# Three expert weight buffers with six gather and twelve sample buffers, in place of two, ten and eight

## The chip, the cores and the metric

The kernel runs on one NeuronCore of a Trainium2 chip. The metric is the device time of one execution in microseconds (us). Ten executions of the kernel before have a median of 6801.84 us and lie between 6792.43 and 6807.85 us.

Five engines work side by side, each through its own instruction queue, in order: PE (TensorE, matrix products and transposes), DVE (VectorE), ACT (ScalarE), POOL (GpSimd, which here issues the indirect DMAs) and SP (SyncE, which issues the plain DMAs). An instruction waits on semaphores for what it needs, and everything behind it on its engine waits with it.

## The reference

Input `x` is (4, 256, 64, 64) in float32. One layer is computed:

```python
x = x + conv_stack(layernorm_over_channels(x))      # three layers, each:
    om   = conv3x3(x, w_off) + b_off                # 27 channels: 18 offsets, 9 masks
    samp = bilinear(x, grid + offsets) * sigmoid(mask)   # 9 taps per position
    x    = relu(einsum('bikhw,oik->bohw', samp, w) + b)  # 9 taps x 256 channels -> 256
t = tokens(x)                                       # (4, 4096, 256)
t = t + ffn(layernorm(t))                           # 8 experts, the best two of each token:
    probs = softmax(t @ gate_w + gate_b); top-2 weights
    y_e   = gelu(t @ W1[e] + b1[e]) @ W2[e] + b2[e]      # 256 -> 512 -> 256
    out   = sum over the two experts of weight * y_e
```

The reference runs all eight experts over all tokens. The kernel runs an expert only on the tokens that chose it.

## The kernel before

**Stages.** A convolution layer of one image is a stage; there are twelve, in the order written out in `run`. A stage has 8 blocks of 512 positions, a block 9 taps, a tap 4 gathers of 128 positions: 288 gathers a stage, 3456 in all. For each gather (`samples`), POOL issues an indirect DMA that brings 128 rows of 4 KB into a gather buffer `g` (L503); DVE makes two weighted sums (L509, then L514 into a sample buffer `s`); ACT scales `s` in place (L517). Two samples are a pair. In `turn`, PE transposes a pair into PSUM (L532) and ACT copies it to `sT` (L535); in `finish`, PE multiplies the four samples of a tap by that tap's weights (L555). A gather buffer is free again when L514 has read it, a sample buffer when PE has transposed it. There are ten of the first (`GB`) and eight of the second (pool `smp`).

**Experts.** When the tokens of an image (a group; the last image has two) are ready, `route` sorts them by expert and cuts them into tiles of 256, so that each tile has one expert: `NF` tiles, 39 for a full group and 23 for a half one, 163 in all. `expert` works one tile off in three pieces. Piece 1: `products` of the tile before (DVE adds the bias that lies in the weight buffer, L892), then PE transposes the tile's tokens (L840) and ACT copies them (L844). Piece 2: first product on PE (L856), and gelu on ACT with a bias that also lies in the weight buffer (L866). Piece 3: second product on PE (L874). At the start of piece 3 (`if beside`), `fetch_next` has POOL issue three indirect DMAs for the next tile: its weights `w` (L800) and two halves of its tokens `zt` (L812). When the kernel drains a lane between or after stages (`self.draining`), the call stands at the start of piece 2 instead. `ffn`, the pool of `zt`, has two buffers.

The weights take 9,232 bytes in each of 128 partitions. If a tile has the same expert as its predecessor, its row numbers are put out of bounds (`same`, L751 to L755) and the DMA moves nothing. The list is walked as two lists, its first half and its second (`order`): even steps take tiles from the first and use weight buffer 0, odd steps from the second, buffer 1.

**Pace.** Lanes mix the pieces into the taps: in a group of pace 5.0 (the first two) a tile goes into 5 taps, at 2.0 into 2 taps, at 1.5 into 1.5; the last group has pace 0. A third lane, `sums`, adds the two expert results to the tokens of the group before: two indirect DMAs `gy` (L915) and two DVE sums (L930) for each 128 tokens. The Tile layer below places each instruction in its engine's order and adds the semaphore waits.

While stage 0 is prepared, `room` also lends gather buffers to the blocks of the input (`xc`, `h`). The `wt` pool, whose two buffers later hold expert weights, lends windows then.

Of the kernel before, what the change touches and what calls it, by code (L numbers as in the profile page):

```python
# [34 lines left out]
FT_LOG = 8  # L35
FT = 1 << FT_LOG
FU = FT // P
GB = 10
LAG = 2
LEAST = 2.0**-30  # L40
WINN = CC * (RPB + 2) * W
W1N = CC * HID + HC
W2N = HC * C + C
# [39 lines left out]
class Group:  # L83


    def __init__(self, b, n0, n1):
        self.b, self.n0, self.n1 = b, n0, n1
        self.nm = f"{b}_{n0}"
        self.M = (n1 - n0) * TPB

        self.NF = 2 * self.M * P // FT + E - 1


        self.half = (self.NF + 1) // 2
        self.zt, self.acc, self.gy, self.sums, self.py = {}, [], [], [], None
        self.order = [s // 2 + s % 2 * self.half for s in range(self.NF)]


class Lane:
# [18 lines left out]
class Weave:  # L118
# [3 lines left out]
    def __init__(self, ctx, tc, ins, out):  # L122
        nc = self.nc = tc.nc
        self.tc = tc
        self.ins = ins
        self.x = ins["x"].rearrange("b (c p) h w -> b p c (h w)", p=P)
        self.out_v = out.rearrange("b (c p) h w -> b p c (h w)", p=P)
        self.B = self.x.shape[0]

        def pool(name, bufs, **kw):  # L130
            return ctx.enter_context(tc.tile_pool(name=name, bufs=bufs, **kw))

        self.cst = pool("cst", 1)
        self.dram = pool("dram", 1, space=bass.MemoryType.DRAM)
        self.wkp = pool("wkp", 1)
        self.plan = pool("plan", 19)
        self.win = pool("win", 3)
        self.wt = pool("wt", 2)
        self.small = pool("small", 1)
        self.big = pool("big", 2)  # L140
        self.ffn = pool("ffn", 2)
        self.rt = pool("rt", 1)
        self.rt2 = pool("rt2", 2)
        self.gyp = pool("gyp", 4)
        self.smT = pool("smT", 2)
        self.smp = pool("smp", 8)
        self.gat = pool("gat", GB)
        self.ps = pool("ps", 3, space=bass.MemoryType.PSUM)
        self.ps1 = pool("ps1", 1, space=bass.MemoryType.PSUM)

        self.routes, self.tiles, self.sums = Lane(), Lane(), Lane()
        self.side, self.plans_side = [], []
        self.last = self.gathered = self.turned = None
        self.starting, self.draining, self.later = True, False, []
        self.pend, self.pairs = None, []
# [534 lines left out]
    def route(self, grp):  # L690

        nc, M, NF = self.nc, grp.M, grp.NF
        grp.slots = self.rt2.tile([P, 2, M], I32, tag="slots", bufs=3, name=f"slots_{grp.nm}")
        grp.tok = self.rt2.tile([P, FU * NF], I32, tag="tok", name=f"tok_{grp.nm}")
        grp.wrow = self.rt2.tile([P, NF], I32, tag="wrow", name=f"wrow_{grp.nm}")

        def small(tag, shape, dt=F32):
            return self.rt.tile(list(shape), dt, tag=tag, name=f"{tag}_{grp.nm}")

        both = small("r0", (P, E, M))  # L700
        nc.vector.tensor_scalar(both, grp.rk, 1.0, None, ALU.is_le)
        rp = self.ps.tile([P, 2, E, M], F32, tag="tp", name=f"rp_{grp.nm}")
        nc.tensor.matmul(rp[:, 0], lhsT=self.upper, rhs=both, start=True, stop=True)
        nc.tensor.matmul(rp[:, 1], lhsT=self.ones, rhs=both, start=True, stop=True)
        tot = small("r1", (P, E, M))
        nc.vector.tensor_copy(tot, rp[:, 1])
        slot = small("r2", (P, E, M))
        nc.vector.tensor_tensor_scan(
            slot.rearrange("p e m -> p (e m)"),
            self.fresh[M].rearrange("p e m -> p (e m)"),  # L710
            tot.rearrange("p e m -> p (e m)"),
            0.0, ALU.mult, ALU.add,
        )

        ni = small("ni", (P, E), I32)
        nc.vector.tensor_scalar(ni, slot[:, :, M - 1], float(FT - 1), None, ALU.add)
        nc.vector.tensor_scalar(ni, ni, FT_LOG, None, ALU.logical_shift_right)
        nt = small("nt", (P, E))
        nc.vector.tensor_copy(nt, ni)
        end = small("end", (P, E))  # L720
        nc.vector.tensor_tensor_scan(end, self.ones[:, :E], nt, 0.0, ALU.mult, ALU.add)
        off = small("off", (P, E))
        nc.vector.tensor_tensor(off, end, nt, ALU.subtract)
        nc.vector.tensor_scalar(off, off, float(FT), None, ALU.mult)
        nc.vector.tensor_tensor(slot, slot, tot, ALU.subtract)
        nc.vector.tensor_tensor(slot, slot, rp[:, 0], ALU.add)
        nc.vector.tensor_tensor(
            slot, slot, off.unsqueeze(2).to_broadcast([P, E, M]), ALU.add
        )
        for i in range(2):  # L730
            mine = small("r0", (P, E, M))
            nc.vector.scalar_tensor_tensor(
                mine, grp.rk, float(i), slot, ALU.is_equal, ALU.mult
            )
            sf = small("sf", (P, M))
            nc.vector.tensor_reduce(sf, mine.rearrange("p e m -> p m e"), AX.X, ALU.add)
            nc.vector.tensor_copy(grp.slots[:, i, :], sf)

        past = small("r1", (P, NF, E))
        nc.vector.tensor_tensor(  # L740
            past,
            self.row_f[:, :NF].unsqueeze(2).to_broadcast([P, NF, E]),
            end.unsqueeze(1).to_broadcast([P, NF, E]),
            ALU.is_ge,
        )
        ex = small("ex", (P, NF))
        nc.vector.tensor_reduce(ex, past, AX.X, ALU.add)
        nc.vector.tensor_scalar(ex, ex, float(E - 1), None, ALU.min)

        rows = small("rows", (P, NF))  # L750
        nc.vector.tensor_scalar(rows, ex, float(P), self.part, ALU.mult, ALU.add)  # L751
        same = small("same", (P, NF))
        nc.vector.tensor_tensor(same[:, 1:], ex[:, 1:], ex[:, : NF - 1], ALU.is_equal)
        nc.vector.memset(same[:, 0 : grp.half + 1 : grp.half], 0.0)
        nc.vector.scalar_tensor_tensor(rows, same, float(E * P), rows, ALU.mult, ALU.add)  # L755
        nc.vector.tensor_copy(grp.wrow, rows)


        grp.digits = []
        for v, (op, k) in enumerate(((ALU.bitwise_and, P - 1), (ALU.logical_shift_right, 7))):  # L760
            di = small("di", (P, 2, M), I32)
            nc.vector.tensor_scalar(di, grp.slots, k, None, op)
            df = small(f"df{v}", (P, 2, M))
            nc.vector.tensor_copy(df, di)
            grp.digits.append(df)
        grp.inv = self.ps1.tile([P, FU * NF], F32, tag="py", name=f"inv_{grp.nm}")
# [23 lines left out]
    def fetch(self, grp, step):  # L790

        if self.w is None:
            self.w = [
                self.wt.tile([P, 2, WINN], F32, tag="wt", name=f"w_{i}").rearrange(
                    "p a b -> p (a b)"
                )
                for i in range(2)
            ]
        f = grp.order[step]
        self.nc.gpsimd.indirect_dma_start(  # L800
            out=self.w[step % 2][:, : W1N + W2N],
            out_offset=None,
            in_=self.ins["W"],
            in_offset=bass.IndirectOffsetOnAxis(ap=grp.wrow[:, f : f + 1], axis=0),
            bounds_check=E * P - 1,
            oob_is_err=False,
        )
        grp.zt[step] = []
        for u in range(FU):
            zt = self.ffn.tile([P, C], F32, tag=f"zt{u}", name=f"zt_{grp.nm}_{f}_{u}")  # L810
            j = FU * f + u
            self.nc.gpsimd.indirect_dma_start(  # L812
                out=zt,
                out_offset=None,
                in_=grp.zd,
                in_offset=bass.IndirectOffsetOnAxis(ap=grp.tok[:, j : j + 1], axis=0),
            )
            grp.zt[step].append(zt)
# [6 lines left out]
    def expert(self, grp, step):  # L825

        nc = self.nc
# [3 lines left out]
        self.products(grp)  # L831
        f = grp.order[step]
        nm = f"{grp.nm}_{f}"
        w = self.w[step % 2]
        w1, w2 = w[:, :W1N], w[:, W1N : W1N + W2N]
        zt = grp.zt.pop(step)
        tp = self.ps.tile([P, CC, FT], F32, tag="tp", name=f"ftp_{nm}")
# [6 lines left out]
        nc.scalar.copy(zT, tp)  # L844
        yield

        beside = not self.draining
        if not beside:
            self.fetch_next(grp, step)
        hT = []  # L850
        for h0 in range(0, HC, 2):
            ph = self.ps1.tile([P, 2, FT], F32, tag="ph", name=f"ph_{nm}_{h0}")
# [13 lines left out]
                nc.scalar.activation(ht[:, h, :], ph[:, h, :], AF.Gelu, bias=w1[:, k : k + 1])  # L866
            hT.append(ht)
        yield
        if beside:
            self.fetch_next(grp, step)  # L870
        py = self.ps1.tile([P, FU, C], F32, tag="py", name=f"py_{nm}")
        for u in range(FU):
            for h in range(HC):
# [262 lines left out]
```

## Time and profile before

The profiled execution took 6800.73 us; its span, from the first to the last instruction, is 6799.0 us.

| what | before |
|---|---|
| median of ten executions | 6801.84 us |
| profiled execution, its span | 6800.73 us, 6799.0 us |
| mean granted TensorE clock | 0.979 |
| PE busy | 6210.4 us (91%) |
| DVE busy | 4963.1 us (73%) |
| ACT busy | 3281.1 us (48%) |
| POOL busy | 4446.6 us (65%), of it L503 3649.4 us |
| DMA | 2223.73 MB; 327 GB/s in the mean |
| weight DMAs issued, of which moved data | 163, 45 |

The 45 are counted from the DMA packets of 9,232 bytes: 5,760, at 128 to a load. "Busy" is time in which an engine executes; "waited for" names what ended its idle time. An engine that idles costs nothing unless the work that it delays is on the path that sets the end.

The stages, as the start of the first gather of each shows them, begin at 93, 614, 1055, 1502, 1961, 2459, 2978, 3508, 4052, 4564, 5074 and 5771 us; the last gather is consumed at 6375 us. Tiles of experts run from 2165 us on: the two groups of pace 5.0 beside stages 4 to 9, that of pace 2.0 beside stage 10, that of pace 1.5 beside stage 11, and the last from 6216 us to about 6740 us.

### The profile page before, as it was taken

How to read it: one execution, taken by the hardware profiler on the slowest of the kernel's cores; microseconds unless marked ns; L12 is line 12 of the kernel's file. 1: busy time of each engine (PE TensorE's matmuls, PEld its weight loads, DVE VectorE, ACT ScalarE, POOL GpSimd, SP SyncE). 2: the span in 40 equal slices, each digit the busy share in tenths (PEclk: the TensorE clock that was granted, in tenths of full speed). 3: DMA queues.
4: the chain of work that ended last, by engine and by line, in shares of the span. 5: the costliest groups of instructions: out<-in, count | busy, mean ns of one | idle time of the engine just before them, and what ended most of it. 6: DMA issues, size and time to landing. Idle time of an engine off the chain costs nothing.

```text
span 6799.0 us, 88985 instructions
## 1 busy us (share of the span) xinstructions
PE 6210.4 (91%) x26500; PEld 3521.5 (52%) x26500; DVE 4963.1 (73%) x11467; ACT 3281.1 (48%) x7141; POOL 4446.6 (65%) x4245
## 2 busy tenths in 40 slices
PE   7998888889999999999999999999998899988987
PEld 3443344444445555555554555555555565755665
DVE  7887778778999676668889777667878555688511
ACT  3554455555555445445554444545554444454322
POOL 4664766766667666666667777666666666677643
PEclk8999999999999999999999999999999999999998
DMA  8998999999999999999998999989998887899744
GB/s 289 349 352 302 365 355 369 357 348 389 382 393 351 329 351 336 322 336 348 356 364 309 363 360 376 322 327 340 353 347 308 290 292 271 293 350 334 245 137 125
DMA packets 800319, 2223.73 MB, mean 327 GB/s; under 512 B 104728, under 2 KB 302872, under 8 KB 794080
## 3 DMA queue, kind: packets, MB, share of 16 engines
q0 software_dynamic: 551200, 1947.35, 77.8%
q1 hardware_dynamic: 248640, 270.69, 11.8%
q8 instruction: 215, 3.52, 0.2%
q14 instruction: 264, 2.16, 0.1%
HBM read 2160.68 MB, written 196.40 MB: 347 GB/s over the span
## 4 chain that ended last, share of the span: by engine, by line
PE 71%; ACT 8%; DMA 7%; DVE 6%; issue 4%; POOL 3%; SPq 0%; ACTq 0%; DVEq 0%; POOLq 0%
PE acc L555 36%; PE tp L532 10%; PE ph L856 7%; PE py L874 7%; PE po L357 7%; DMA g<-tab,idx 5%; ACT sT L535 3%; DVE g L509 2%; ACT s L517 2%; DVE s L514 2%; POOL g L503 1%; POOL gy L915 1%; PE pm L371 1%; ACT win L577 1%; PE ftp L840 1%
## 5 line engine op out<-in xcount | busy, mean ns | idle before, releaser
L503 POOL DMA_INDIRECT g<-tab,idx x3456 | 3649.4, 1056 | 1792.7 <-DVE s L514 642.7
L555 PE MATMUL acc<-sT,wk 128*128 128x512 f32 x6912 | 3386.7, 604 | 151.9 <-ACT sT L535 137.1
L509 DVE SCALAR_TENSOR_TENSOR g<-g,cf 128x512 f32<-128x512 f32 x3456 | 2560.9, 743 | 393.1 <-DMA g<-tab,idx 388.5
L514 DVE SCALAR_TENSOR_TENSOR s<-g,cf 128x256 f32<-128x256 f32 x3456 | 1661.7, 483 | 753.5 <-PE tp L532 469.0
L535 ACT COPY sT<-tp 128x512 f32<-128x512 f32 x1728 | 1001.4, 586 | 1820.8 <-PE tp L532 1814.0
L517 ACT ACTIVATE s<-s,cf 128x256 f32<-128x256 f32 x3456 | 1641.2, 508 | 435.0 <-DVE s L514 398.3
L555 PEld LDWEIGHTS acc<-sT,wk 128*128 128x128 f32 x6912 | 1161.0, 192 | 967.0 <-issue 655.4
L532 PEld LDWEIGHTS tp<-ident,s 128*128 128x128 f32 x6912 | 882.4, 143 | 1350.8 <-issue 651.2
L532 PE MATMUL tp<-ident,s 128*128 128x128 f32 x6912 | 1252.8, 281 | 189.3 <-ACT s L517 171.8
L856 PE MATMUL ph<-fzT,w 128*128 128x256 f32 x2608 | 682.6, 394 | 60.6 <-ACT fzT L844 36.1
L874 PE MATMUL py<-w,hT 128*128 128x256 f32 x2608 | 653.1, 389 | 31.3 <-ACT hT L866 26.1
L856 PEld LDWEIGHTS ph<-fzT,w 128*128 128x128 f32 x2608 | 481.4, 195 | 188.0 <-ACT fzT L844 63.5
L874 PEld LDWEIGHTS py<-w,hT 128*128 128x128 f32 x2608 | 475.2, 192 | 164.7 <-ACT hT L866 69.1
L866 ACT ACTIVATE hT<-ph,w 128x256 f32<-128x256 f32 x652 | 282.2, 471 | 455.9 <-PE ph L856 436.8
L812 POOL DMA_INDIRECT zt<-z,tok x326 | 334.6, 1026 | 161.1 <-issue 86.1
L357 PE MATMUL po<-win,wo 128*32 128x504 f32 (+1 forms) x2304 | 356.6, 597 | 5.5 <-ACT win L301 3.2
L800 POOL DMA_INDIRECT w<-in_W,wrow x163 | 176.7, 1084 | 268.0 <-issue 97.7
L915 POOL DMA_INDIRECT gy<-ys,slots x256 | 262.2, 1024 | 109.8 <-issue 63.0
L892 DVE TENSOR_TENSOR y<-py,w 128x512 f32<-128x512 f32 x163 | 111.7, 685 | 220.6 <-PE py L874 220.6
L930 DVE SCALAR_TENSOR_TENSOR ta<-gy,cw,ta 128x256 f32<-128x256 f32 x256 | 120.6, 480 | 135.9 <-DMA gy<-ys,slots 77.1
L357 PE MATMUL po<-win_pre,wo 128*32 128x504 f32 (+1 forms) x1152 | 185.3, 621 | 2.0 <-ACT om L366 2.0
L357 PEld LDWEIGHTS po<-win,wo 128*32 128x32 f32 x2304 | 73.0, 109 | 177.0 <-issue 141.7
(154 smaller groups left out, 2927.9 us busy)
## 6 DMA issues: line engine op xcount, KB each, us to landing
tab<-hv SPq DMA_DIRECT2D x512, 128.0 KB
g<-tab,idx POOLq DMA_INDIRECT x3456
ys<-y SPq DMA_DIRECT2D x163, 256.0 KB
tab<-h_pre SPq DMA_DIRECT2D x128, 256.0 KB
wk<-in_conv_w SPq DMA_DIRECT2D x99, 256.0 KB
xc_pre<-in_x SPq DMA_DIRECT2D x32, 512.0 KB
xr_tok<-in_x SPq DMA_DIRECT2D x32, 512.0 KB
t<-t_tok SPq DMA_DIRECT2D x32, 512.0 KB
```

What stands on the lines that cost most here:

```text
L357: nc.tensor.matmul(po[g * Q : (g + 1) * Q, :].rearrange("q (r w) -> q r w", w=W)[:, :, x0:x1], lhsT=self.wo[l][:, 3 * ky + kx, c, :], rhs= ...
L503: self.gathered = nc.gpsimd.indirect_dma_start(out=g.rearrange("p x s f -> p (x s f)"), out_offset=None, in_=self.table(*self.stages[i]), ...
L509: nc.vector.scalar_tensor_tensor(g[:, :, 0, :], g[:, :, 1, :], cf[:, j, 0:1], g[:, :, 0, :], ALU.mult, ALU.add,)
L514: self.last = nc.vector.scalar_tensor_tensor(s, g[:, 1, 0, :], cf[:, j, 1:2], g[:, 0, 0, :], ALU.mult, ALU.add)
L517: nc.scalar.activation(s, s, AF.Copy, scale=cf[:, j, 2:3])
L532: self.turned = nc.tensor.transpose(tp[:, c, u * P : (u + 1) * P], ss[u][:, c * P : (c + 1) * P], self.ident)
L535: nc.scalar.copy(self.sT[:, :, t0 * P : (t0 + 2) * P], tp)
L555: nc.tensor.matmul(acc[:, o, :], lhsT=self.wk[k][:, c, o * P : (o + 1) * P], rhs=sT[:, c, :], start=(k == 0 and c == 0), stop=(k == K - 1 ...
L812: self.nc.gpsimd.indirect_dma_start(out=zt, out_offset=None, in_=grp.zd, in_offset=bass.IndirectOffsetOnAxis(ap=grp.tok[:, j : j + 1], axi ...
L856: nc.tensor.matmul(ph[:, h, :], lhsT=w1[:, o : o + P], rhs=zT[:, c, :], start=(c == 0), stop=(c == CC - 1),)
L874: nc.tensor.matmul(py[:, u, :], lhsT=hT[h // 2][:, h % 2, u * P : (u + 1) * P], rhs=w2[:, h * C : (h + 1) * C], start=(h == 0), stop=(h == ...
L915: self.nc.gpsimd.indirect_dma_start(out=g, out_offset=None, in_=self.ys[grp.i % 3], in_offset=bass.IndirectOffsetOnAxis(ap=grp.slots[:, i, ...
```

## The change

The list of a group's tiles is walked as three thirds instead of two halves, with a weight buffer for each; the row numbers are valid again at the start of each third. `fetch_next` is called at the start of piece 2 always. The gather buffers go from ten to six, the sample buffers from eight to twelve.

```diff
-GB = 10
+GB = 6
@@ class Group
-        self.half = (self.NF + 1) // 2
+        self.third = -(-self.NF // 3)
-        self.order = [s // 2 + s % 2 * self.half for s in range(self.NF)]
+        self.order = [s // 3 + s % 3 * self.third for s in range(self.NF)]
@@ class Weave
-        self.wt = pool("wt", 2)
+        self.wt = pool("wt", 3)
-        self.smp = pool("smp", 8)
+        self.smp = pool("smp", 12)
@@ def route
-        nc.vector.memset(same[:, 0 : grp.half + 1 : grp.half], 0.0)
+        nc.vector.memset(same[:, 0 : 2 * grp.third + 1 : grp.third], 0.0)
@@ def fetch
-                for i in range(2)
+                for i in range(3)
-            out=self.w[step % 2][:, : W1N + W2N],
+            out=self.w[step % 3][:, : W1N + W2N],
@@ def expert
-        w = self.w[step % 2]
+        w = self.w[step % 3]
@@ def expert, start of piece 2
-        beside = not self.draining
-        if not beside:
-            self.fetch_next(grp, step)
+        self.fetch_next(grp, step)
@@ def expert, start of piece 3
-        if beside:
-            self.fetch_next(grp, step)
```

In bytes of a partition, four gather buffers less are 16,384, four sample buffers more 4,096, and the third buffer of the `wt` pool 10,240.

## The prediction

> **What bounds the kernel now.** I read the busy shares first (PE 91%, DVE 73%, POOL 65%), then the busy times by stage, because the mean hides that the stages differ, and then the waits inside the stages that stand out. Columns of the first view: stretch in us, its length, busy time and instructions of PE, PEld, DVE, ACT and POOL, granted clock, DMA share, GB/s.
>
> ```profile
> 582.00:1064.00 482.00, 420.60 (x1683) 189.68 (x1681) 360.95 (x742) 232.29 (x514) 311.52 (x295) 0.99 0.92 341
> 1513.00:1975.00 462.00, 422.86 (x1793) 221.22 (x1793) 426.24 (x1134) 247.96 (x547) 315.13 (x290) 0.97 1.01 387
> 5090.00:5746.00 656.00, 591.88 (x2539) 371.66 (x2537) 428.07 (x946) 297.71 (x636) 432.77 (x413) 0.96 0.84 295
> 5746.00:6375.00 629.00, 583.94 (x2505) 381.17 (x2505) 455.80 (x1069) 306.32 (x642) 436.68 (x415) 0.98 0.89 318
> 6375.00:6799.00 424.00, 337.87 (x1506) 266.09 (x1504) 96.67 (x262) 96.58 (x214) 186.63 (x191) 0.89 0.45 138
> ```
>
> PE is the bound nearly everywhere. Stage 3 (second line) has three engines near full at once: PE 92%, DVE 92%, DMA 1.01. In stages 10 and 11 (third and fourth) PE idles 109.2 of 1285 us, 8.5%; in stages 4 to 9 (1975 to 5090 us, PE busy 2939.3) it idles 175.7 of 3115, 5.6%. The waits of stages 10 and 11 say why; the last two lines are from the tail after 6375 us.
>
> ```profile
> DVE g L509 <- DMA g<-tab,idx: 283.2, 145, 10.5
> POOL w L800 <- ACT s L517: 52.7, 18, 4.8
> POOL w L800 <- ACT hT L866: 30.7, 10, 5.2
> POOL w L800 <- ACT sT L535: 13.2, 5, 4.4
> ...
> PE ph L856 <- DMA w<-in_W,wrow: 20.7, 7, 7.5
> PE ftp L840 <- DMA zt<-z,tok: 3.1, 2, 1.8
> ```
>
> DVE waits for gathers (283 of its 388 us in the whole run), and POOL is held at the weight DMA. All rows of L800 there but "issue" sum to 124 us over 40 waits, 3.1 each. The timeline shows one:
>
> ```profile
> 5335.67 0.95 POOL L503 DMA_INDIRECT g<-tab,idx  x1 [0.30 <-issue]
> ...
> 5337.86 0.75 DVE L509 SCALAR_TENSOR_TENSOR g<-g,cf 128x512 f32<-128x512 f32 x1 [7.08 <-DMA g<-tab,idx]
> ...
> 5343.97 0.68 DVE L892 TENSOR_TENSOR y<-py,w 128x512 f32<-128x512 f32 x1
> ...
> 5345.44 1.47 POOL L800 DMA_INDIRECT w<-in_W,wrow  x1 [4.75 <-ACT s L517]
> ```
>
> POOL cannot issue the weight DMA until DVE has read the bias out of that buffer (5343.97); eight gathers and two gy are queued behind it.
>
> **The third buffer and the earlier fetch.** At pace 2.0 a tile step takes 20.1 us (21 steps from 5324 to 5747) and POOL issues 13 DMAs in it: 8 gathers, w, two zt, two gy, at 0.96 + 0.30 us, 16.4 us. With the wait of 3 to 4.75 us this is the step. PE needs 592/656 of it, 18.1 us. So POOL's wait, not PE, sets the step.
>
> With two buffers, the fetch for tile s+1 waits for L892 of tile s-1: two pieces back, 1.3 taps or 5 gathers at pace 2.0. With three it waits for tile s-2, four pieces back even though it is issued a piece earlier. In the built programs the instruction waited for stands some 35 places ahead of the DMA before, over 170 after. zt, now the nearer wait (L840 of tile s-1, four pieces back instead of five), has two buffers still; four pieces at pace 1.5 are two taps, 8 gathers. I take both as free while POOL's lead is at most 6. What that relief is worth: if stages 10 and 11 idle like stages 4 to 9, 1175.8/0.9436 = 1246 us, **-39 us**; the bounds are 0 and -109, all of PE's idle time there. That the lead is then held by the gather buffers instead keeps me from going above -39.
>
> In the tail, fetch_next stood at piece 2 already; only the buffer counts. A load that moves data is issued when L892 of s-2, not s-1, is done: a tile earlier, and a tile there takes 8.2 us (L892 at 6507.03, 6515.23, 6523.42). The longest wait is 7.5, so all should go: **-24 us** (20.7 + 3.1). Bounds: 0 (zt waits for L840, 48.0 us on POOL, stand in front of w in the queue) and -40, with PE's weight-load waits of 12.6 and 3.6 counted as separate.
>
> In stages 4 to 9 POOL's largest row at L800 is 15.4 us of "issue", in 49 waits: nothing to gain.
>
> **Thirds.** Each group has one more break, so up to 5 loads more than 45, each 128 packets of 348 ns on 16 engines, 2.8 us: 14 us of DMA. A load now has three pieces of lead (16 us at pace 2.0). **+3 us**, bounds 0 and 14; without that cover it is PE at L856 that waits. The other DMAs of a step and the memset are unchanged in number.
>
> **Six gather buffers.** Gather j now waits for L514 of gather j-6; behind it on POOL stand the next gathers, w, zt and gy, and DVE waits for those. I took, for each of the 3456 gathers, its issue, its landing (its semaphore's last update) and its consumption. Issue to landing is 6.7 us at the median, 5.1 at the fast end (5%), 10.0 at 95%. A turn of one buffer is 0.3 + 6.7 + 1.3 (L509 0.74, L514 0.48) = 8.3 us; over six buffers 1.4 us per gather, against a cadence of 1.55 (stages 1 and 2) to 2.3 us (stage 10). So it holds in the mean, barely. Stage 3 has a mean landing of 8.25: (8.25 + 1.6)/6 = 1.64 against 1.59; it does not hold there.
>
> [...]
>
> How much a late gather costs: moving each issue to 0.25 us after the consumption of j-6 and keeping its landing time, 840 gathers land after DVE asked, in 171 runs of neighbours; adding only the largest delay of each run, DVE is late by 244 us in all. Most is covered: in stages 0, 1, 2, 5, 8 and 9 DVE finishes a sample 9.1 to 10.6 us (median) before ACT scales it, and 0 to 3.5 us per stage come through. In stages 3, 4 and 6, where that slack is 1.4, 8.7 and 4.7, 25.2 + 8.2 + 6.2 come through: **+39 us**. The 11 us of the other stages I leave to the four samples more. One place in stage 10 (5246 us, 26 us) I leave out: DVE was held there by full sample buffers, and it now has four more. Bounds: 0, and 244 if no cover holds.
>
> **Twelve sample buffers.** They let DVE run four further ahead: DVE waits 469 us at L514 for PE to free a sample. Up to the first expert tiles the built order of PE and ACT is the same as before, and ACT there waits for PE, not DVE. I take **0**, as what keeps the cover above; bounds -44 (a third of the 131 us that PE waits for ACT's s outside stages 10 and 11) and 0. Together ten plus eight and six plus twelve hold the same 18 gathers between POOL and PE.
>
> **The start.** Fewer lent buffers: SP's loads wait for buffers used three blocks earlier. Taken at 0; bounds 0 and +9, one round from load to load (24.12 to 33.16 us).
>
> **Sum.** 6800.7 - 39 - 24 + 3 + 39 = 6780 us for the profiled execution, which lies 1.1 us under the median; **6780 us**, 0.3% faster. Less than 0.2% (13.6 us) I call no change.
>
> **The rivals.** *Six buffers bind (slower).* In stages 0 to 9, gather landing replaces the sample buffers as what holds DVE: when POOL has issued w, zt, zt (3.8 us) it has no lead of ten left to repay them. For it: the thin 1.4 against 1.55, the DMA at 0.92 to 1.01. Against: 9 us of slack before ACT. It decides once more than 60/244, a quarter, of DVE's delay reaches the end; at half, 122 us, 6801 - 60 + 122 = 6863.
> *Cancelled (no change).* PE at 90 to 93% in stages 10 and 11 takes little of POOL's freed time, because the gather wait takes the place of the weight wait there; only the tail pays: 6801 - 24 + 3 + 20 = 6800.
> *More gain.* The sample buffers also give back a third of PE's waits and the six hold: 6801 - 63 - 44 + 13 = 6707.
> *It doesn't do what it says*: POOL is held at zt instead of w, since zt still has two buffers. Then the first term is 0 and it is the slow rival at its mildest, 6820; I count it there.
>
> **How the numbers follow.** Forecast 0.42 (6750 to 6800: 0.37 faster, 0.05 same); more gain 0.07; cancelled 0.14 (0.10 same, 0.04 slower); binding 0.37, of it 0.01 same. Faster 0.44, same 0.16, slower 0.40: cases of both signs hold most, so the forecast's own range stands beside the whole one. That leaves out the fastest half of "more gain" and the far end of binding: 6710 to 6880.
>
> **What would show it.** L800's waits on POOL in stages 10 and 11 fall from 124 us to under 30 and the step there from 20.1 to about 19.4; PE's wait for w in the tail is gone; L509's wait for gathers rises in stages 3, 4 and 6 and stays below the slack elsewhere, with stages 0, 1 and 2 as long as before. I am wrong if stages 1 and 2 grow by over 5 us each (binding), or if stage 10 keeps its 656 us while L800's waits are gone (cancelled).

## The result, and the profile after

| | before | after |
|---|---|---|
| median of the runs taken side by side | 6801.57 us (30 runs) | 6839.07 us (9 runs) |
| ratio, 95% interval | | 1.0052 [1.0044, 1.0061] |
| profiled span, granted clock | 6799.0 us, 0.979 | 6837.7 us, 0.975 |
| loads of `w` that moved data (packets of 9,232 bytes / 128) | 45 | 47 |

The change is slower by 0.5%, 37.5 us by the medians; 6780 us had been forecast. In the sets of runs of the experiments below the kernel before took about 6805 us in two sets and about 7505 us in five, so a kernel is compared only with the kernel before of its own set.

The same three stretches as before (stage 3, stages 10 and 11 together, the tail), in the view of busy times by stretch of the changed kernel; columns as before:

```profile
1514.00:1999.00 485.00, 431.85 (x1783) 227.21 (x1782) 428.35 (x1125) 250.55 (x545) 314.28 (x289) 0.94 0.99 366
5166.00:6435.00 1269.00, 1183.55 (x5074) 755.38 (x5074) 898.45 (x2030) 597.72 (x1285) 887.77 (x840) 0.97 0.90 316
6435.00:6838.00 403.00, 333.48 (x1508) 265.16 (x1506) 96.38 (x262) 98.13 (x217) 180.07 (x186) 0.91 0.46 144
```

Stage 3 grew from 462 to 485 us and its clock fell from 0.97 to 0.94. Stages 10 and 11 shrank from 1285 to 1269 us, the tail from 424 to 403.

What DVE waits for, from the costliest groups, first of the kernel before, then of the changed one (busy, mean ns of one, idle before, and what ended most of it):

```profile
L509 DVE SCALAR_TENSOR_TENSOR g<-g,cf 128x512 f32<-128x512 f32 x3456 | 2560.9, 743 | 393.1 <-DMA g<-tab,idx 388.5
L514 DVE SCALAR_TENSOR_TENSOR s<-g,cf 128x256 f32<-128x256 f32 x3456 | 1661.7, 483 | 753.5 <-PE tp L532 469.0
```

```profile
L509 DVE SCALAR_TENSOR_TENSOR g<-g,cf 128x512 f32<-128x512 f32 x3456 | 2568.5, 745 | 645.8 <-DMA g<-tab,idx 633.6
L514 DVE SCALAR_TENSOR_TENSOR s<-g,cf 128x256 f32<-128x256 f32 x3456 | 1663.7, 483 | 402.4 <-PE tp L532 105.0
```

DVE's idle time has changed its cause: 364 us less for PE to free a sample, 245 us more for a gather to land. A wait for PE is harmless, since PE is the bound (busy 92% of the changed kernel's span); a wait for a gather can be harmful. The sum over the run doesn't say which; the stages do.

The waits in stages 10 and 11 of the changed kernel (engine and line, what ended the wait: us in total, times, longest):

```profile
DVE g L509 <- DMA g<-tab,idx: 169.8, 148, 7.0
...
POOL g L503 <- DVE s L514: 78.2, 52, 6.3
...
POOL w L800 <- ACT hv L328: 14.3, 1, 14.3
POOL w L800 <- issue: 14.3, 30, 4.4
...
POOL w L800 <- ACT s L517: 1.2, 4, 0.3
```

POOL no longer stands at the weight DMA: the rows of L800 other than "issue" are 25 us in place of 124. It stands at the gather buffers more, 78.2 us where it was 25.1. In the tail PE's wait at the first product for `w` (20.7 us before) has no row left.

**Cutting the stages.** The prediction cut the run at the first gather of each stage. That mark moves with POOL's lead: by it stage 1 grew by 10 us. I now cut where ACT copies (L535) the last pair of a stage, which is PE's own progress, and use this cut from here on. In us, one profiled execution of each kernel against one of the kernel before; the kernels of the last four columns are experiments, named by their gather, sample and weight buffers:

| stage | before | after | 6 gather, 12 samples | 6 gather, 8 samples | 9, 8, third `w` | 9, 8, third `w`, fetch at piece 3 |
|---|---|---|---|---|---|---|
| 0 to 2 | 1520.0 | +4.1 | +0.7 | +0.1 | -3.1 | +0.1 |
| 3 | 459.5 | +23.3 | +25.8 | +25.9 | -4.0 | +0.3 |
| 4 | 502.0 | +11.7 | +10.1 | +8.0 | -0.6 | 0.0 |
| 5 | 519.4 | +6.6 | -0.3 | -1.6 | +2.9 | 0.0 |
| 6 | 523.9 | +10.8 | +6.4 | +5.6 | +7.2 | +0.3 |
| 7 | 540.8 | +15.2 | +11.7 | +13.8 | +5.6 | +0.4 |
| 8 | 522.4 | +4.4 | +2.4 | +1.3 | +1.5 | +0.3 |
| 9 | 505.4 | +10.2 | +5.3 | +7.0 | +9.1 | +3.7 |
| 10 | 654.2 | -29.8 | +5.2 | +9.7 | -33.1 | -33.6 |
| 11 | 633.6 | +6.5 | +12.6 | +13.2 | -10.5 | -11.4 |
| tail | 417.8 | -24.3 | -2.1 | +1.9 | -21.6 | -25.7 |
| span | 6799.0 | +38.7 | +77.7 | +84.9 | -46.5 | -65.6 |

### The profile page after: what moved, and what is told of

It is laid out like the page before. It is cut to its first block, busy times and chain, and to the rows that moved or that the text cites. A ratio compares the mean times of both kernels' runs of the same rounds, so it can differ in the third digit from the quotient of the medians.

```text
span 6837.7 us, 89185 instructions
## 1 busy us (share of the span) xinstructions
PE 6259.4 (92%) x26500; PEld 3535.7 (52%) x26500; DVE 5029.1 (74%) x11467; ACT 3281.2 (48%) x7141; POOL 4459.3 (65%) x4245
## 3 DMA queue, kind: packets, MB, share of 16 engines
q1 hardware_dynamic: 248640, 270.69, 11.7%
## 4 chain that ended last, share of the span: by engine, by line
PE 67%; DMA 10%; DVE 8%; ACT 8%; issue 4%; POOL 3%; SPq 0%; ACTq 0%; DVEq 0%; POOLq 0%
PE acc L555 33%; PE tp L532 9%; DMA g<-tab,idx 8%; PE py L870 7%; PE ph L854 7%; PE po L357 6%; ACT sT L535 3%; DVE g L509 3%; DVE s L514 2%; POOL g L503 2%; ACT s L517 2%; PE pm L371 1%; PE ftp L840 1%; PE tpv L325 1%; ACT win L577 1%
## 5 line engine op out<-in xcount | busy, mean ns | idle before, releaser
L555 PE MATMUL acc<-sT,wk 128*128 128x512 f32 x6912 | 3436.6, 609 | 158.9 <-ACT sT L535 155.3
L509 DVE SCALAR_TENSOR_TENSOR g<-g,cf 128x512 f32<-128x512 f32 x3456 | 2568.5, 745 | 645.8 <-DMA g<-tab,idx 633.6
L514 DVE SCALAR_TENSOR_TENSOR s<-g,cf 128x256 f32<-128x256 f32 x3456 | 1663.7, 483 | 402.4 <-PE tp L532 105.0
L535 ACT COPY sT<-tp 128x512 f32<-128x512 f32 x1728 | 1004.1, 586 | 1943.8 <-PE tp L532 1937.6
L517 ACT ACTIVATE s<-s,cf 128x256 f32<-128x256 f32 x3456 | 1639.0, 508 | 431.4 <-DVE s L514 402.4
L555 PEld LDWEIGHTS acc<-sT,wk 128*128 128x128 f32 x6912 | 1169.0, 193 | 943.6 <-issue 624.5
L532 PEld LDWEIGHTS tp<-ident,s 128*128 128x128 f32 x6912 | 889.1, 144 | 1429.5 <-issue 690.2
L532 PE MATMUL tp<-ident,s 128*128 128x128 f32 x6912 | 1278.8, 283 | 186.1 <-ACT s L517 174.9
L854 PE MATMUL ph<-fzT,w 128*128 128x256 f32 x2608 | 658.9, 387 | 21.9 <-ACT fzT L844 17.3
L812 POOL DMA_INDIRECT zt<-z,tok x326 | 336.7, 1033 | 139.5 <-issue 65.6
L800 POOL DMA_INDIRECT w<-in_W,wrow x163 | 178.1, 1092 | 173.0 <-issue 78.4
```

The source lines that it names most:

```text
L509: nc.vector.scalar_tensor_tensor(g[:, :, 0, :], g[:, :, 1, :], cf[:, j, 0:1], g[:, :, 0, :], ALU.mult, ALU.add,)
L514: self.last = nc.vector.scalar_tensor_tensor(s, g[:, 1, 0, :], cf[:, j, 1:2], g[:, 0, 0, :], ALU.mult, ALU.add)
L517: nc.scalar.activation(s, s, AF.Copy, scale=cf[:, j, 2:3])
L532: self.turned = nc.tensor.transpose(tp[:, c, u * P : (u + 1) * P], ss[u][:, c * P : (c + 1) * P], self.ident)
L535: nc.scalar.copy(self.sT[:, :, t0 * P : (t0 + 2) * P], tp)
L555: nc.tensor.matmul(acc[:, o, :], lhsT=self.wk[k][:, c, o * P : (o + 1) * P], rhs=sT[:, c, :], start=(k == 0 and c == 0), stop=(k == K - 1 ...
```

## The experiments

The experiments measured beside some 6805 us for the kernel before tell about the forecast and come first; the others have a part of their own below.

**Six gather and twelve sample buffers alone.** Against the kernel before:

```diff
-GB = 10
+GB = 6
-        self.smp = pool("smp", 8)
+        self.smp = pool("smp", 12)
```

> The kernel of the run with six and twelve again, since in the first set the kernel before itself took 7510 us, with idle times of several us on every engine that no semaphore explains. Theory (six gather buffers cost all of the loss): 1.2 to 1.4% slower than before, stages 1 to 9 longer by about 92 us, stage 10 and the tail as before. Rival (thirds and early fetch cost 53 us): 0.6% slower, only stages 1 to 3 longer.

Measured: 6881.89 us beside 6804.16, ratio 1.0118 [1.0101, 1.0135], some 80 us. Stages 3, 4 and 6 grew by 42.3 us, stages 7 to 9 by 19.4, stages 10 and 11 by 17.8, and stages 0 to 2 by 0.7. Stages 1 to 9 together grew by 62.8 us, a third less than expected, and stages 10 and 11 were not as before. Still these two edits alone cost twice what the whole change lost, and gain nothing where the weight buffer gains.

How a late gather reaches PE shows in the timeline of this kernel in stage 3 (start, duration, engine and line, operation, and in brackets the idle time before it with what ended it):

```profile
1713.51 0.75 DVE L509 SCALAR_TENSOR_TENSOR g<-g,cf 128x512 f32<-128x512 f32 x1 [1.76 <-DMA g<-tab,idx]
...
1714.77 0.16 DVE L68 TENSOR_SCALAR ve_pre<-mv_pre 128x4 f32<-128x4 f32 x1
...
1715.12 0.94 POOL L503 DMA_INDIRECT g<-tab,idx  x1 [2.58 <-DVE ve_pre L68]
...
1720.04 1.38 DVE L78 TENSOR_SCALAR h_pre<-h_pre,mv_pre,rs_pre 128x256 f32<-128x256 f32 x4
1720.20 1.07 POOL L503 DMA_INDIRECT g<-tab,idx  x1 [0.79 <-DVE rs_pre L75]
1720.51 1.75 PE L462 MATMUL tp_pre<-ident,h_pre 128*128 128x128 f32 x7 [5.70 <-DVE h_pre L78]
```

DVE waits 1.76 us for a gather. Behind it in DVE's order stand not only samples, which have slack, but the small steps of the next image's normalization (`ve_pre`, `rs_pre`, `h_pre`), which PE transposes at L462 as soon as they are there. They come late, and PE idles 5.70 us. The waits of the whole stage 3, of the kernel before and then of this one:

```profile
PE tp_pre L462 <- DVE h_pre L78: 19.4, 7, 3.6
...
PE tp L532 <- ACT s L517: 3.7, 8, 1.1
```

```profile
PE tp_pre L462 <- DVE h_pre L78: 37.0, 7, 6.8
DVE g L509 <- DMA g<-tab,idx: 34.9, 42, 2.2
...
PE tp L532 <- ACT s L517: 6.9, 15, 1.1
```

Once in each block the wait for `h_pre` is some 2.5 us longer, 17.6 us in all; PE's wait for samples (L517), which the prediction counted, grew by 3.2 us only.

The clock then adds to it: before, the records show one stretch of 3.4 us at half clock (granted 0.5) at each such place (at 1650, 1708, 1766, 1824, 1882 and 1941 us), now one of 6.8 us (1657, 1718, 1780, 1841, 1902 and 1964 us). Over the whole run the records at half clock sum to 290.1 us before and 361.5 us here. In such a stretch an L555 matmul of this kernel takes 1062 ns in the median, outside 593. Idle time in a stretch costs nothing more; PE is busy in 204.7 us of them before and in 261.2 here, and with half of that taken as lost, an estimate of 102 and 131 us, the clock accounts for 28 of the 78 us. PE's idle time over the whole run, half clock or not, grew by 44.7 us; some 5 us are left.

In the kernel before and in the changed one the shortest and the median stretch at half clock last 3.41 us. At the start of the six stretches before, or up to 1.5 us ahead of it, PE idles 2.5 to 3.1 us at five and 3.6 us at the sixth; in the place above it idles 5.70 us. How long an idle time it takes to bring such a stretch is not shown.

The same kernel in another set:

> The kernel before with six gather and twelve sample buffers; two weight buffers, halves and the late fetch stay. Theory (six gather buffers cost all of the loss): stages 1 to 9 grow by about 92 us together as in the changed kernel, stage 10 and the tail keep their 697 and 424 us; 6885 to 6900 us in all. Rival (the walk in thirds and the earlier fetch cost what stages 4 to 9 lost, 53 us): only stages 1 to 3 grow, by 39 us; about 6841 us.

It took 7530.94 us beside 7510.43 for the kernel before, ratio 1.0030 [1.0003, 1.0057].

**Six gather buffers with eight samples.** Only `GB = 6` against the kernel before; it asks what the four samples more are worth.

> The kernel before with six gather buffers alone, on whichever of the two kinds of chip it meets. Where the kernel before takes some 6800 us: if twelve samples cover part of the late gathers, stages 1 to 9 grow by 80 to 140 us (ratio 1.012 to 1.02); if they cover nothing, by 64 to 84 us (1.011 to 1.013); if they are harmful, by less than 60 us (below 1.009). Where it takes some 7500 us: about 0.99 again.

Measured: 6899.52 us beside 6805.92, ratio 1.0147 [1.0129, 1.0166]. The ratio and the stages disagree about the samples. The ratio is 0.0029 above that of the run with twelve, give or take 0.0025, some 20 us, and lies where the expectation says that the samples cover part. In the profiled executions stages 1 to 9 grow by 62.8 us with eight samples and by 62.8 us with twelve, close to "cover nothing"; stage 10 and the tail are 4 to 5 us longer each with eight. But the profiled execution with eight is the fastest of its four, and a stage is seen in one execution only. So whether the four samples more cover nothing or some 20 us stays open. Either way 78 us come through with twelve of them.

**Nine gather, eight sample and three weight buffers.** These fit as well: they take 6,144 bytes of a partition more than the buffers of the kernel before, so the third weight buffer did not need the step down to six. Against the changed kernel:

```diff
-GB = 6
+GB = 9
-        self.smp = pool("smp", 12)
+        self.smp = pool("smp", 8)
```

> The kernel of the run with nine, eight and three again, for the same reason. Theory: 0.7 to 0.9% faster than before, with the gain in stage 10 and the tail (58 us) and stages 1 to 9 within 10 us of before. Rival (thirds and early fetch cost 53 us in stages 4 to 9): within 0.2% of before.

Measured: 6759.02 us beside 6804.16, ratio 0.9943 [0.9926, 0.9960]. Stages 10 and 11 and the tail keep the gain (-65.2 us together), stages 3 and 4 no longer grow, and DVE's wait for gathers is 232.6 us, less than the 388.5 before. The gain is smaller than the 0.7 to 0.9% expected, since stages 5 to 9 are 26.3 us longer than before.

**The same with the fetch at piece 3.** The third buffer stays, the earlier fetch goes. Against the kernel just above:

```diff
+        beside = not self.draining
+        if not beside:
+            self.fetch_next(grp, step)
-        self.fetch_next(grp, step)
...
+        if beside:
+            self.fetch_next(grp, step)
```

> Third weight buffer, nine gather and eight sample buffers, fetch at piece 3 beside a stage. Where the kernel before takes some 6800 us: if the buffer alone gives the gain, stages 10, 11 and tail together stay 50 to 65 us under it and the ratio is 0.990 to 0.994; if the earlier fetch gives it, only the tail's 23 us remain and the ratio is 0.995 to 0.999. Where it takes some 7500 us: 0.998 again.

Measured: 6737.68 us beside 6805.92, ratio 0.9906 [0.9890, 0.9923]. This beats both kernels: 0.9% faster than before. The view of busy times for stage 3, stages 10 and 11, and the tail of this kernel, and rows of its waits in stages 10 and 11:

```profile
1504.00:1966.00 462.00, 421.65 (x1789) 219.95 (x1788) 425.28 (x1120) 247.62 (x546) 314.20 (x290) 0.97 1.01 387
5078.00:6331.00 1253.00, 1173.81 (x5094) 753.36 (x5092) 885.75 (x2034) 598.91 (x1295) 882.03 (x840) 0.98 0.90 321
6331.00:6734.00 403.00, 334.04 (x1523) 265.89 (x1521) 96.31 (x262) 98.14 (x218) 181.32 (x187) 0.91 0.47 145
```

```profile
DVE g L509 <- DMA g<-tab,idx: 98.3, 62, 6.4
...
POOL w L800 <- ACT hv L328: 14.5, 2, 14.2
POOL w L800 <- ACT s L517: 11.4, 8, 9.3
```

The rows of L800 other than "issue" are 34 us without the earlier fetch, in place of 124 before, so it is the buffer that removes most of the wait. Stages 10 and 11 and the tail are 70.7 us shorter than before, more than the 50 to 65 expected. DVE waits 98.3 us for gathers in place of 283.2, because POOL isn't held in front of them. Stage 3 is as before to 0.3 us, stages 4 to 8 to 0.4, although this kernel walks its list in thirds and loads weights 47 times: the thirds cost nothing that shows.

The difference to the kernel above it is the price of the early fetch: 25 us by the ratios (0.0037 of 6806 us, give or take 0.0024; the intervals are just apart), 19 us by the spans. Of the 19 some 6 may be the measure: where nothing disturbs them the same transposes (L532) last 272.8 ns in the one profiled execution and 272.6 in the other. The kernel before, though, took no longer beside the first (6804.16 us) than beside the second (6805.92). The price falls into stages 5 to 9, 22 us, beside the tiles of pace 5.0, where the prediction found no wait at L800 to remove. PE's idle time there is the same (149.5 us with the early fetch, 148.4 without). Of its long matmuls of the convolution (L555) 47 touch a stretch at half clock, against 16, and the PE instructions that touch one take 33.4 us above their medians, against 23.2. That the early fetch costs is shown, if not how much; why more matmuls meet the half clock, and where the other half of the 22 us lies, is not.

## The same kernels where the kernel before takes 7500 us

There the order is another one. Each ratio is to the kernel before of the same set; nothing here bears on the 37.5 us.

| kernel | ratios |
|---|---|
| 6 gather, 8 samples | 0.9886, 0.9890, 0.9907 |
| 9, 8, third `w`, fetch at piece 3 | 0.9979, 0.9978, 0.9976 |
| 6 gather, 12 samples | 1.0030 |
| 9, 8, third `w`, early fetch | 1.0096, 1.0088, 1.0066 |
| 6, 12, third `w`, fetch at piece 3 | 1.0102, 1.0104 |
| 8, 12, third `w`, early fetch | 1.0281 |
| 10 gather, 12 samples | 1.0347 |

The intervals are 0.15 to 0.4% to each side. Six gather buffers with eight samples, three times:

> The kernel before with six gather buffers and the eight sample buffers that it had. If the four sample buffers more cover part of the late gathers, this is slower than the run with six and twelve by 10 to 40 us, and DVE waits at L514 for PE again (469 us before). If they cover nothing, the two are within 10 us.

> The kernel of the run with six and eight again (two weight buffers), on a chip where before takes about 6800 us. If the four sample buffers more cover part of the late gathers, it is slower than the 1.0118 of six and twelve by 0.2 to 0.6%, and DVE waits at L514 for PE (sample buffers) and at L509 (gathers). If they cover nothing, it is within 0.2% of 1.0118.

> The kernel before with six gather buffers alone (eight samples kept). My theory: DVE is held by late gathers because only six gather buffers are in the air, and a larger stock of finished samples covers some of it; so stages 1 to 9 grow by at least the 74 us that six and twelve cost, 80 to 140 us, and the ratio to the kernel before is 1.012 to 1.02. Rival one: the samples cover nothing, the growth is the same 74 us within 10 and the ratio 1.011 to 1.013. Rival two: twelve samples are harmful in themselves (DVE runs further ahead and asks for gathers earlier), then six and eight are better than six and twelve: ratio below 1.009.

They took 7418.68, 7430.35 and 7441.63 us beside 7510.43, 7500.16 and 7504.94: 1% faster, where the same kernel is 1.5% slower beside 6805.92. None of the theories above had that; rival two of the last expectation has the ratio, but beside 6805.92 six and eight are no better than six and twelve.

Nine, eight and three with the early fetch:

> The changed kernel (three weight buffers, thirds, early fetch) with nine gather and eight sample buffers, which fit beside them. Theory: the gain of stage 10 and the tail (58 us) stays, the loss goes but for a few us of the tenth buffer; 6745 to 6760 us. Rival (thirds and early fetch cost 53 us in stages 4 to 9): about 6798 us.

> Nine gather and eight sample buffers, three weight buffers, the earlier fetch. If the earlier fetch costs some 20 us also here, the ratio stays at 0.993 to 0.995, where the same kernel with the fetch at piece 3 had 0.9906. If the difference came from the two chips that the two kernels met, the ratio is 0.990 to 0.992.

> Nine gather and eight sample buffers, three weight buffers, the earlier fetch, for a chip on which the kernel before takes some 6800 us. If the earlier fetch costs some 20 us: ratio 0.993 to 0.995. If the difference to the fetch at piece 3 came from the chips: 0.990 to 0.992. Where the kernel before takes some 7500 us: 1.009 again.

7578.66, 7579.72 and 7564.99 us. And with the fetch at piece 3:

> As the run with nine, eight and three, but the fetch is at the start of piece 3 outside the drains, as it was before. If the third buffer alone frees POOL, within 10 us of that run. If the earlier fetch is needed as well, stage 10 keeps most of its 697 us and this is 25 to 40 us slower than that run.

> The kernel of the run with nine, eight, three and the late fetch again. If the third buffer alone frees POOL, within 0.15% of the 0.9943 of the early fetch, stage 10 near 666 us. If the early fetch is needed as well, 0.4 to 0.6% slower than that, stage 10 near 690 us.

> The changed kernel with nine gather and eight sample buffers and the fetch put back to piece 3 beside a stage; the third weight buffer stays. My theory: the third buffer alone gives the gain, because L800 then waits for a tile two back; stages 10 and 11 and the tail stay together 50 to 65 us under the kernel before, and stages 5 and 8, which grew by 8 and 11 us with the early fetch, return to within 4 us; ratio to the kernel before 0.990 to 0.994. Rival: the earlier fetch gives the gain; then stages 10 and 11 are within 10 us of the kernel before, the tail still 23 us shorter (there the fetch stood at piece 2 in both), and the ratio is 0.995 to 0.999.

7492.14, 7482.93 and 7490.43 us. The early fetch costs here too, about 1%. That 0.9976 lies in the rival's range of the last expectation says nothing for it: the same kernel had 0.9906 beside 6805.92, with stages 10 and 11 shorter by 45 us.

The changed kernel with the fetch put back to piece 3 and nothing else; it was to show the price of the early fetch beside six gather buffers:

> The changed kernel with nothing but the fetch put back to piece 3 beside a stage. My theory: the earlier fetch costs some 20 us by itself, whatever the buffers are; then this kernel is the sum of six and twelve alone (+78) and the third weight buffer alone (-66), 12 us over the kernel before, ratio 1.000 to 1.003 where the changed kernel had 1.0052. Rival: with six gather buffers the earlier fetch costs nothing, because POOL is held by the gathers anyway; ratio 1.0045 to 1.006. A second rival: with six gather buffers the earlier fetch is needed, because POOL then reaches the fetch later; ratio above 1.006.

> The changed kernel with the fetch put back to piece 3 beside a stage, for a chip on which the kernel before takes some 6800 us. If the earlier fetch costs some 20 us whatever the buffers are: ratio 1.000 to 1.003. If it costs nothing with six gather buffers: 1.0045 to 1.006. If it is needed there: above 1.006. Where the kernel before takes some 7500 us: 1.010 again.

7592.86 and 7587.32 us. Beside about 6805 us this kernel was not measured, so the price of the early fetch beside six gather buffers stays open. Twelve samples alone against the kernel before, and eight gather buffers against the changed kernel:

```diff
-        self.smp = pool("smp", 8)
+        self.smp = pool("smp", 12)
```

```diff
-GB = 6
+GB = 8
```

> The kernel before with twelve sample buffers and nothing else. The prediction's term: no change, 1.000 within 0.002, though DVE's wait for PE at L514 (469 us) falls. Rival: samples are what PE waits for, and a third of that wait comes back, 44 us, 0.9935.

> The changed kernel with eight gather buffers instead of six. Theory: one buffer's turn is 8.3 us, over eight 1.04 us a gather, below DVE's own 1.23, so that L509's wait for gathers in stages 1 to 9 falls under 100 us (after: 429) and the time is that of nine and eight, 0.994 within 0.0015. Rival (it is the count of buffers between POOL and DVE that must cover the 3.8 us of the three expert DMAs, and eight is still short): 0.998 to 1.000.

7769.85 and 7707.59 us, 3.5% and 2.8% slower, the worst two, and the two with the most buffers in both pools together (22 and 20; six and eight, the best, have 14). Both expectations missed. Neither was measured beside 6805 us, so whether twelve samples beside ten gather buffers cost or gain there is open.

## Why the prediction was wrong

The three parts of the change, each from its own runs, add up: +80 (six and twelve, ratio 1.0118), -64 (third buffer, 0.9906) and +25 (early fetch) make +41 us, where the change measured +37.5. The sum takes the early fetch to cost beside six gather buffers what it costs beside nine. In the table of stages the columns of six and twelve and of nine, eight and a third `w` add up to +31.2, in no row more than 7 us from the column of the change. Against these, step by step:

- **"The third buffer and the earlier fetch", -39, and the tail, -24.** The buffer is right in mechanism: L800's waits fell from 124 to 25 us, and beside nine gather buffers stages 10 and 11 gained 45.0 us and the tail 25.7. The first term was mis-sized to the safe side: the mean of the first 20 tile steps of pace 2.0, from one bias sum of DVE to the next, fell from 20.1 to 17.8 us, not to 19.4. In the changed kernel only 23.3 of the 45.0 reach the end in stages 10 and 11. The six gather buffers alone cost 17.8 us there, and DVE waits there 169.8 us for gathers, where it waits 98.3 with nine buffers.
- **The earlier fetch beside stages 4 to 9.** This step failed: the prediction looks there for what the fetch could gain, finds "nothing to gain", and has no term for what it could lose, although 78 tiles lie there. It cost some 25 us by the ratios, against nothing in the sum.
- **"Six gather buffers", +39.** This step failed by half: some 78 us were measured. The three stages that were charged with 25.2, 8.2 and 6.2 us measured 25.8, 10.1 and 6.4. What failed is the sentence after the count, "The 11 us of the other stages I leave to the four samples more": in stages 5 and 7 to 11, 36.9 us came through with the four samples in place. That they would cover was an assumption with no row behind it, and the working itself said that both pairs of pools hold the same 18 gathers. To add the 11 and the 26 us of the one place in stage 10 back would give 77, but not by place: stage 10 grew by 5.2 us, stages 7, 9 and 11 by 29.6.
- **That the count met the size in stages 3, 4 and 6 is partly luck.** It charged DVE's delay after ACT's slack. The runs show another way in stage 3: DVE's small steps for the next image, which have no slack, are late, and then more of PE's work falls into half clock. The clock, an estimate of 28 of the 78 us, is a term that the prediction didn't have; 18 of the 28 fall into stages 5 and 7 to 11. In stage 9 PE idles no longer than before, and the clock, an estimate of 6 us, is all that the trace shows for its 5.3 us.
- **"Stages 0, 1 and 2 as long as before".** Right: +0.7 us together with six and twelve alone, and 4.1 in the changed kernel, though DVE's wait for gathers there rose from 14 to 83 us (stages 0 to 2 by their gathers). There the samples do have some 9 us of slack. The test that was set ("stages 1 and 2 grow by over 5 us each") would have been misread at the first gather of a stage, +10 and +3.
- **Thirds, +3.** Two loads more, not five; no cost shows.
- **Twelve samples, 0.** Between six and eight and six and twelve lie 0 us in stages 1 to 9 by the profiled executions and some 20 us by the ratios; the sum has them as 0 here and as cover above.

The rival *Six buffers bind (slower)* was right that gather landing takes over as what holds DVE, and its price was too high: the loss is 80 us, a third of DVE's 244, above its point of a quarter and below the half at which 6863 was worked out. The reason that it gives, "when POOL has issued w, zt, zt (3.8 us) it has no lead of ten left", can't hold in stage 3, where a third of the loss lies and no tile is worked on yet; there a mean landing of 8.25 us was already too long for six buffers by the prediction's own 1.64 against 1.59. Nor do they bind in the stages of the fastest cadence (1 and 2), but most in stage 3, where DVE also does work that PE waits for at once. *Cancelled* has the right mechanism in stages 10 and 11, the gather wait in place of the weight wait, but only half of the gain went there. *More gain* fell, since the six didn't hold. *It doesn't do what it says* fell too: behind `zt`, which has two buffers still, POOL waits 7.5 us for PE's transposes in stages 10 and 11.

## What to carry to other kernels

A count of delays is worth what its last subtraction is worth: before a part of it is left to some cover, look for the row that shows the cover, and for everything else that stands behind the delayed instruction on the same engine, small steps above all. When several edits come as one because they share a room, ask of each whether it is needed: here the third weight buffer alone, with nine and eight, fits and gives 0.9906, and the early fetch and the six buffers only take from it. Compare stages at a mark of the engine that bounds them; a mark on an engine that runs ahead moves with its lead.

## What was not expected of the hardware

The kernel before, unchanged, took 6804 and 6806 us in two sets of the experiments and 7500 to 7514 us in five, 10% more, with the runs of a set within 1% of each other. The number of the chip doesn't tell the sets apart: it was 6 in one of each kind. In the long kind the same instructions last as long (the median L555 matmul takes 592 ns in both; L509, L514 and L535 take 0.74, 0.48 and 0.59 us in the timeline of the kernel with ten and twelve, and 743, 483 and 586 ns in the mean before), but engines idle until an event that the profile can put down to no instruction and no DMA ("remote"): 818 us in the kernel with six and twelve, none in the kernel before or after where these take some 6800 us. The longest such rows in the waits of the kernel with ten and twelve (span 7775.8 us; the same view's columns as above):

```profile
ACT sT L535 <- remote: 532.4, 117, 14.9
...
DVE s L514 <- remote: 190.3, 68, 13.3
```

The mean granted clock of the profiled executions is lower too: 0.927 here and 0.953 in the fastest kernel of that kind (six and eight), against 0.974 to 0.982 for all kernels in the other kind. With the fetch left where it was, the fewer buffers POOL and DVE have to run ahead in, the faster a kernel is there: 0.989 to 0.991 with 14 in both pools, 0.998 with 17, 1.000 to 1.010 with 18, 1.035 with 22. What the engines wait for stays open.
